# A graph attention layer on one core: differences of destinations, from two GpSimd subtractions to twenty-one ScalarE activations

## The chip, the core and the metric

The kernel runs on one core of a Trainium2 chip. The metric is the device time of one execution in microseconds. The engines are named as in the profile: PE (TensorE, matrix products), DVE (VectorE), ACT (ScalarE), POOL (GpSimd) and SP (SyncE, which here only issues DMA transfers). Each engine works through its own list of instructions in order; semaphores make it wait for another engine or for a transfer. The 16 DMA engines serve the queues of all issuers. The gathers by index are issued by POOL, which spends time on each; nearly all other transfers are issued by SP.

## What is computed

There are 12,500 nodes with 128 features and 400,000 edges, sorted by destination, with 32 features each. Cut to what matters:

```python
h = relu(layernorm(x))                       # no weights
def layer(x, src, dst, edge_attr):           # x is h; 8 heads of 16 channels
    y = ln(x, ln1_g, ln1_b)
    x_l, x_r, e = y @ W_l, y @ W_r, edge_attr @ W_e
    m = leaky_relu(x_l[src] + x_r[dst] + e, 0.2)
    alpha = einsum('ehc,hc->eh', m, att)     # softmax over the edges of a destination
    a = softmax_by(dst, alpha)
    h2 = x + segment_sum(x_l[src] * a, dst) + bias
    return h2 + gelu(ln(h2, ln2_g, ln2_b) @ W1 + b1) @ W2 + b2
out = x + layer(h, src, dst, edge_attr)
```

Each node also has an edge to itself, whose features are the mean over all edges. Everything is float32, except where the kernel uses bf16 for numbers that fit it or for parts of numbers.

## The kernel before, in words

Nodes are taken in 25 quads: 24 of four tiles of 128 nodes, and a last one of two tiles. Edges are taken in 782 pairs. A pair is two units, a unit is 256 edges.

**The node phase** (lines 690 to 744) is a software pipeline of 35 rounds. In each round a table of stages runs for different quads: x_stats (DVE) for quad r, relu (ACT) for quad r-3, h_turn (PE) for r-4, h_square (ACT) and the copy out of PSUM for r-5 (even quads by ACT, odd by DVE), product (PE) for r-7, and x_l (DVE, then a store to xl_dram by SP) for r-8. The rows of x_l stand in three SBUF buffers in turn (xls), so the x_l of a quad waits until the store of three quads before has landed. At the head of a round stand a reciprocal (DVE) for the roots of two rounds ago and a square root (ACT) for those of the last round. first_xr does the same for x_r of the first quad, one step a round from round 8 on; two of its steps are L580 and L586 on DVE. All is recorded in program order, and this order is kept on each engine: nothing is rescheduled.

**Raw gathers.** 24 of the edge pairs get their source rows in another way: in the node phase POOL gathers rows of the input x for them (raw_gather, L270, four gathers of 128 rows a pair), SP stores them in raw_dram (raw_store, L278, three rounds on), and in the edge phase they are turned into rows of x_l. The round of each is in rows_at (L720): 5/4 of its number, and three rounds more from the tenth on. There are five raw tiles in turn, so a gather waits for the store of five pairs before. The position in rows_at does not change the order on POOL, which has nothing else to do here except the subtractions; it sets where the stores stand in SP's list among the stores of x_l (L535).

**Differences.** The edge phase places edges by the difference of their destination from the first destination of their unit, and from that of their pair. dc holds all destinations, 112 partitions of 3,584 (14 units, or 7 pairs) and a few beyond. In round 12 from_first converts them to float32 (L389) and POOL takes both sets of differences, each in one instruction over the whole tile with the first destinations broadcast (L393); SP stores each in DRAM (L399). In round 14 fits (L401) tests on DVE whether the windows used later suffice and sets a flag, by which the kernel chooses between the edge phase described here and a general one.

**The edge phase** (window_edges) runs 782 rounds. For each pair POOL gathers four blocks of 128 rows of xl_dram (gather, L896), four rounds ahead, into 12 buffers; SP loads edge features, differences (dlw, L913) and a window of x_r; DVE compares differences with a column (L924); PE forms the sum z, ACT and DVE bend it, PE and DVE and ACT make scores and weights, and PE sums weighted rows. Finished nodes are normalised and put through the feed-forward part between rounds. Before its first gather POOL clears six buffers (L875). As these lie in memory that the node phase used, and as the gathers read xl_dram, the node phase's gathers and the stores to xl_dram have to have landed by then.

Of the kernel before, what the change touches and what calls it, by code (L numbers as in the profile page):

```python
# [13 lines left out]
F32 = mybir.dt.float32  # L14
BF16 = mybir.dt.bfloat16
I32 = mybir.dt.int32
AF = mybir.ActivationFunctionType
OP = mybir.AluOpType
# [16 lines left out]
U = KU * P  # L35
UP = 2
QP = 4
RU = 14
# [80 lines left out]
def raw_pairs(nt, n_edges):  # L119

    n_pr = -(-n_edges // (UP * U))
    at = [xr_round(t, nt, n_edges) + XR_STEPS + 1 for t in range(GN, nt, GN)]
    return [(r + RAW_STEPS + AHEAD + 1, r) for r in at if r + RAW_STEPS + AHEAD + 2 < n_pr]
# [11 lines left out]
def tile_gnn(  # L135
# [23 lines left out]
    nc = tc.nc  # L159
# [8 lines left out]
    RP = -(-NU // RU)  # L168
# [12 lines left out]
    dc_dram = dram.tile([RP * RU * U], BF16, name="dc_dram")  # L181
    du_dram = dram.tile([RP * RU * U], BF16, name="du_dram")
    raw = [{"c": c, "i": i, "round": r, "n": UP * KU} for i, (c, r) in enumerate(raw_pairs(NT, n_edges))]
# [36 lines left out]
    rng = pre.enter_context(tc.tile_pool(name="rng", bufs=1))  # L220
# [9 lines left out]
    EP = RU * U  # L230
# [4 lines left out]
    def load_weights():  # L235
        nc.scalar.dma_start(wl_sb, w_l)
        nc.scalar.dma_start(wr_sb, w_r)
        nc.scalar.dma_start(g1_c, column(ln1_g))
        nc.scalar.dma_start(b1n_c, column(ln1_b))

    def load_consts():
        for i, v in enumerate((ln2_g, ln2_b, None, b1[0:P], b1[P : 2 * P])):
            if v is not None:
                nc.sync.dma_start(cols[:, 2 + i : 3 + i], column(v))
        nc.sync.dma_start(att_c, bass.AP(tensor=att.tensor, offset=att.offset, ap=[[1, C], [C, H], [1, 1]]))
        nc.sync.dma_start(we_sb, bass.AP(tensor=w_e.tensor, offset=w_e.offset, ap=[[P, DE], [0, QP], [1, P]]))
        nc.sync.dma_start(w1_sb, w1)
        nc.sync.dma_start(w2_sb, w2.rearrange("(k p) f -> p k f", p=P))
        nc.sync.dma_start(bias_r, row_bcast(bias, P))
        nc.sync.dma_start(b2_r, row_bcast(b2, P))  # L250
        nc.sync.dma_start(src_sb, src)
        nc.sync.dma_start(first_sb, bass.AP(tensor=dst.tensor, offset=dst.offset, ap=[[0, 1], [U, NU]]))
# [3 lines left out]
    def load_raw():  # L256
        step = raw[1]["c"] - raw[0]["c"]
        assert all(d["c"] == raw[0]["c"] + i * step for i, d in enumerate(raw))
        nc.sync.dma_start(
            src_raw,  # L260
            bass.AP(
                tensor=src.tensor, offset=src.offset + raw[0]["c"] * UP * KU,
                ap=[[NCH * K, P], [step * UP * KU, len(raw)], [1, UP * KU]],
            ),
        )

    def raw_gather(d):
        d["x"] = node.tile([P, UP * KU, P], F32, name="raw", bufs=5)
        for j in range(d["n"]):
            nc.gpsimd.indirect_dma_start(  # L270
                out=d["x"][:, j, :],
                out_offset=None,
                in_=x,
                in_offset=bass.IndirectOffsetOnAxis(ap=src_raw[:, d["i"], j : j + 1], axis=0),
            )

    def raw_store(d):
        nc.sync.dma_start(raw_dram[d["i"], :, 0 : d["n"], :], d["x"][:, 0 : d["n"]])  # L278

    def load_x(t0, n):  # L280
        if n > 0:
            nc.sync.dma_start(h_sb[:, t0 : t0 + n, :], x_t[:, t0 : t0 + n, :])  # L282

    def load_dst():
        nc.gpsimd.memset(dc[:, EP : EP + U + 1], NO_NODE)
        if rest < EP:
            nc.gpsimd.memset(dc[(RP - 1) // DE * DE :, rest:EP], NO_NODE)
        if RP > 1:
            over = min(EP + U + 1, NCH * CE - (RP - 2) * EP)
            nc.sync.dma_start(  # L290
                dc[0 : RP - 1, 0:EP], bass.AP(tensor=dst.tensor, offset=dst.offset, ap=[[EP, RP - 1], [1, EP]])
            )
            nc.sync.dma_start(
                dc[RP - 2 : RP - 1, EP:over],
                bass.AP(tensor=dst.tensor, offset=dst.offset + (RP - 1) * EP, ap=[[0, 1], [1, over - EP]]),
            )
            if RP > 2:
                nc.sync.dma_start(
                    dc[0 : RP - 2, EP : EP + U + 1],
                    bass.AP(tensor=dst.tensor, offset=dst.offset + EP, ap=[[EP, RP - 2], [1, U + 1]]),  # L300
                )
        nc.sync.dma_start(dc[RP - 1 : RP, 0:rest], dst[(RP - 1) * EP :].rearrange("(o e) -> o e", o=1))
        nc.gpsimd.memset(lu, NO_NODE)
        if RP > 1:
            nc.sync.dma_start(
                lu[0 : RP - 1, :], bass.AP(tensor=dst.tensor, offset=dst.offset + U - 1, ap=[[EP, RP - 1], [U, RU]])
            )
        nc.sync.dma_start(
            lu[RP - 1 : RP, 0 : rest // U],
            bass.AP(tensor=dst.tensor, offset=dst.offset + (RP - 1) * EP + U - 1, ap=[[0, 1], [U, rest // U]]),  # L310
        )

        u = NUE - 1
        nc.sync.dma_start(
            lu[u // RU : u // RU + 1, u % RU : u % RU + 1],
            bass.AP(tensor=dst.tensor, offset=dst.offset + n_edges - 1, ap=[[0, 1], [1, 1]]),
        )
# [27 lines left out]
    def count_up():  # L345
        iota(nc, nh, [[-1, H], [-H, NW]], 0, 1)
        iota(nc, own, [[-1, NW], [0, H]], -NC3, 1)
        iota(nc, last, [[0, NW], [0, H]], -NC3 - NW, 1)
        iota(nc, third, [[-NS, CW]], 0, 1)
        iota(nc, in_order, [[1, CW]])  # L350
        iota(nc, unit, [[0, 1]], -NC3, 1)
        iota(nc, fq, [[-1, QP], [-QP, DE]], 0, 1)
        iota(nc, place, [[1, RU]], 0, RU)
        iota(nc, fh, [[-1, H], [-H, C]], 0, 1)
# [29 lines left out]

    df = rng.tile([RP, EP + U + 1], F32, name="df")
    bad = rng.tile([RP, 2], F32, name="bad")

    def from_first():
        nc.vector.tensor_copy(df, dc)  # L389
        for step, to in ((U, du_dram), (UP * U, dc_dram)):  # L390
            de = df[:, 0:EP].rearrange("p (u e) -> p u e", e=step)
            dlb = rng.tile([RP, EP], BF16, name="dlb", bufs=2)
            nc.gpsimd.tensor_tensor(  # L393
                dlb.rearrange("p (u e) -> p u e", e=step),
                de,
                de[:, :, 0:1].to_broadcast([RP, EP // step, step]),
                op=OP.subtract,
            )
            nc.sync.dma_start(to.rearrange("(p e) -> p e", e=EP), dlb)  # L399

    def fits():  # L401
# [44 lines left out]
    qs = [  # L446
        {"t0": t, "n": n, "ts": slice(t, t + n), "h": h_sb[:, t : t + n, :], "mean": mean_sb[:, t : t + n]}
        for t, n in quads
    ]
# [253 lines left out]
    LAST = 8  # L703
    first_xr = xr_steps(node, lambda: once_ps.tile([P, GN * P], F32, name="w_ps"))
    with tc.manual_schedule():
        make_identity(nc, ident)
        count_up()
        for t in xls:
            nc.gpsimd.memset(t[:, :, P:], 1.0)
        load_weights()  # L710
        load_x(0, min(GN, NT))
        load_raw()
        load_x(GN, min(3 * GN, NT - GN))
        for t in range(4 * GN, NT, 14):
            load_x(t, min(14, NT - t))
        load_dst()
        load_consts()
        nc.gpsimd.memset(empty, 0.0)
        nc.gpsimd.memset(empty[:, :, C + 1 : SH], CAP)
        rows_at = [i * 5 // 4 + (3 if i >= 10 else 0) for i in range(len(raw))]  # L720
        for r in range(max(max(len(qs), 9) + LAST + 1, rows_at[-1] + 4)):
            for d, at in zip(raw, rows_at):
                if r == at:
                    raw_gather(d)
                if r == at + 3:
                    raw_store(d)
            if r == 3:
                weights()
            if r == 7:
                edge_constants()  # L730
            if r == 12:
                from_first()
            if r == 14:
                fits()
            for t in slots(r - 2):
                nc.vector.reciprocal(t, t)
            for t in slots(r - 1):
                nc.scalar.activation(t, t, AF.Sqrt)
            for late, f in node_stages:
                if 0 <= r - late < len(qs):  # L740
                    f(qs[r - late], r)
            if 0 <= r - LAST < len(first_xr):
                first_xr[r - LAST](qs[0])
        clear(0)
# [952 lines left out]
```

## Time and profile before

| | |
|---|---|
| time, median of 3 runs | 4050.42 us (4048.72 to 4051.7) |
| profiled execution, its own time | 4055.89 us |
| its span, first to last instruction | 4053.7 us |
| mean granted clock of TensorE | 0.955 |
| busy: PE, DVE, ACT, POOL | 3555.2 us (88%), 2539.5 (63%), 2135.2 (53%), 2984.9 (74%) |
| chain that ended last: PE, POOL, DMA | 40%, 24%, 22% of the span |
| DMA traffic | 560.85 MB, mean 138 GB/s |
| the two subtractions of L393 | 12.3 us on POOL, at 100.5 and 106.7 us |
| raw gathers (L270) | 96 of 995 ns on average |
| edge gathers (L896) | 3029, 949 ns on average |

The rows that the profile gives for groups of instructions name a line, an engine, an operation and a tile, then count, busy time, the mean of one in ns, and the idle time of the engine just ahead of them with what ended it ("issue" where the profile shows no wait). A timeline row is the start in us, the duration in us, engine, line, operation, output and input; in square brackets stands the idle time ahead of it and who ended it. Start-to-start distances are of more use than durations where instructions of an engine overlap a little. Rows with SPq are transfers as SP issues them: their duration is that of issuing, not of the transfer.

### The profile page before, as it was taken

The numbers are of one execution on the slowest core, as the hardware profiler recorded it, in microseconds if no ns is written. First come the engines' busy times: TensorE is split into PE (matmuls) and PEld (weight loads), VectorE is DVE, ScalarE is ACT, GpSimd is POOL, SyncE is SP. The second block draws the span as 40 slices with busy tenths as digits, with TensorE's granted clock in tenths as the row PEclk, the third lists the DMA queues.
The fourth block names the chain that finished last, engine by engine and source line by source line (L and its number), as shares of the span: only waits on it lengthen the run. The fifth ranks groups of instructions, "written<-read, shape, count | busy, mean of one in ns | idle before, by whom it ended". The sixth has DMA issues, their size and how long they took to land.

```text
span 4053.7 us, 65778 instructions
## 1 busy us (share of the span) xinstructions
PE 3555.2 (88%) x19254; PEld 2501.5 (62%) x19255; DVE 2539.5 (63%) x5834; ACT 2135.2 (53%) x4638; POOL 2984.9 (74%) x3156
## 2 busy tenths in 40 slices
PE   2388888998989999999999999999989999989986
PEld 2356665665666666666666666666766666666664
DVE  5656665766666666666666666666666665666654
ACT  4544444544445555565455556555555555545543
POOL 4777777777777777777777777777777777777772
PEclk6699999999999999999999999999999999999998
DMA  5668878777766666656665665656666666565562
GB/s 160 198 165 198 185 194 197 171 163 165 172 124 126 126 124 131 123 121 129 132 125 124 128 129 120 136 123 117 124 136 126 124 130 128 107 135 114 120 134 50
DMA packets 648212, 560.85 MB, mean 138 GB/s; under 512 B 386387, under 2 KB 525506, under 8 KB 647602
## 3 DMA queue, kind: packets, MB, share of 16 engines
q1 hardware_dynamic: 547266, 339.01, 33.7%
q0 software_dynamic: 100000, 217.41, 30.2%
q8 instruction: 156, 2.56, 0.3%
q14 instruction: 214, 1.75, 0.2%
q10 hardware_dynamic: 576, 0.13, 0.0%
HBM read 489.81 MB, written 66.32 MB: 137 GB/s over the span
## 4 chain that ended last, share of the span: by engine, by line
PE 40%; POOL 24%; DMA 22%; issue 13%; SPq 1%; DVE 0%; ACT 0%; POOLq 0%; DVEq 0%; ACTq 0%
POOL xs L896 22%; DMA xs<-xl_dram,src_sb 21%; PE z L942 9%; PE acc L1000 8%; PE ab L960 7%; PE pt_ps L986 4%; PE z L938 4%; PE z L941 2%; PE ab L959 2%; POOL raw L270 2%; PE acc L1233 1%; PE acc L1208 1%; DMA lu<-in_dst 1%; SPq L282 0%; DMA state<-rec 0%
## 5 line engine op out<-in xcount | busy, mean ns | idle before, releaser
L896 POOL DMA_INDIRECT xs<-xl_dram,src_sb x3029 | 2873.0, 949 | 923.2 <-issue 796.0
L978 ACT ACTIVATE p<-ab,rec 128x256 f32<-128x256 f32 x1563 | 656.8, 472 | 1056.5 <-DVE rec L967 1044.3
L1009 DVE TENSOR_TENSOR own<-acc,diag 128x272 f32<-128x272 f32 x782 | 344.1, 440 | 1068.5 <-PE acc L1000 1039.6
L938 PE MATMUL z<-ident,xs 128*128 128x128 f32 x3125 | 573.3, 283 | 353.0 <-DMA xs<-xl_dram,src_sb 318.3
L938 PEld LDWEIGHTS z<-ident,xs 128*128 128x128 f32 x3125 | 399.5, 142 | 772.3 <-DMA xs<-xl_dram,src_sb 434.5
L1000 PE MATMUL acc<-xs,pt 128*128 128x136 f32 x6250 | 874.9, 284 | 0.2 <-DVE f_yo L1247 0.2
L942 PE MATMUL z<-ea,we_z 128*128 128x512 f32 x1564 | 835.4, 617 | 0.0
L1000 PEld LDWEIGHTS acc<-xs,pt 128*128 128x128 f32 x6250 | 802.6, 195 | 0.4 <-PE pt_ps L986 0.4
L960 PE MATMUL ab<-m,negrep 128*128 128x512 f32 x1564 | 801.4, 594 | 0.0
L991 ACT COPY pt<-pt_ps 128x512 f32<-128x512 f32 x782 | 455.9, 583 | 623.3 <-PE pt_ps L986 611.5
L986 PEld LDWEIGHTS pt_ps<-ident,p 128*128 128x128 f32 x3125 | 407.8, 146 | 438.2 <-issue 386.4
L967 DVE TENSOR_REDUCE rec<-ab 128x2 f32<-128x512 f32 x781 | 540.2, 692 | 123.4 <-PE ab L960 113.2
L953 DVE TENSOR_TENSOR m<-z,zs 128x512 f32<-128x512 f32 x782 | 533.0, 682 | 115.0 <-ACT zs L948 114.7
L948 ACT ACTIVATE zs<-z 128x512 f32<-128x512 f32 x782 | 472.2, 604 | 41.4 <-DMA dlw<-dc_dram 33.6
L986 PE MATMUL pt_ps<-ident,p 128*128 128x128 f32 x3125 | 489.2, 281 | 2.2 <-ACT pt L991 1.3
L1015 DVE TENSOR_REDUCE rec<-own 128x34 f32<-128x272 f32 x782 | 340.9, 436 | 26.7
L942 PEld LDWEIGHTS z<-ea,we_z 128*128 128x128 f32 x1564 | 306.5, 196 | 32.5
L960 PEld LDWEIGHTS ab<-m,negrep 128*128 128x128 f32 x1564 | 300.6, 192 | 37.1 <-issue 1.2
L941 PE MATMUL z<-ne,xrw 128*128 128x512 bf16 x782 | 304.0, 389 | 0.2 <-DMA xs<-xl_dram,src_sb 0.2
L959 PE MATMUL ab<-ne,farw 128*128 128x512 bf16 x782 | 299.6, 383 | 0.0
L924 DVE TENSOR_SCALAR ne<-dlw,nid 112x512 bf16<-112x512 bf16 x782 | 289.8, 371 | 13.0 <-DMA dlw<-du_dram 13.0
L270 POOL DMA_INDIRECT raw<-in_x,src_raw x96 | 95.5, 995 | 71.3 <-DMA raw_dram<-raw 40.1
(198 smaller groups left out, 2235.6 us busy)
## 6 DMA issues: line engine op xcount, KB each, us to landing
dlw<-dc_dram SPq DMA_DIRECT2D x196, 384.0 KB
ea<-in_ea_t SPq DMA_DIRECT2D x196, 256.0 KB
ea_s<-in_ea_t SPq DMA_DIRECT2D x98, 512.0 KB
xs<-xl_dram,src_sb POOLq DMA_INDIRECT x3029
state<-rec SPq DMA_DIRECT2D x1563, 9.0 KB
xrw<-xs_dram SPq DMA_DIRECT2D x782, 24.0 KB
state<-empty SPq DMA_DIRECT2D x28, 504.0 KB
st<-state SPq DMA_DIRECT2D x48, 288.0 KB
```

Of the source, the lines that this page charges most:

```text
L896: nc.gpsimd.indirect_dma_start(out=xs[:, j, :], out_offset=None, in_=xl_dram, in_offset=bass.IndirectOffsetOnAxis(ap=src_sb[:, c * KP + j ...
L938: nc.tensor.matmul(z[:, j * P : (j + 1) * P], d["xs"][:, j, 0:P], ident, start=(j == 0), stop=False, is_transpose=True)
L941: nc.tensor.matmul(z[:, :e], xrw[c % NV], d["ne"][:, :e], start=False, stop=False)
L942: nc.tensor.matmul(z[:, :e], we_z[:, c % QP, :], d["ea"][:, :e], start=False, stop=True)
L948: nc.scalar.activation(d["zs"][:, :e], d["z"][:, :e], AF.Copy, scale=SLOPE)
L953: nc.vector.tensor_tensor(d["m"][:, :e], d["z"][:, :e], d["zs"][:, :e], op=OP.max)
L960: nc.tensor.matmul(ab[:, :e], negrep.rearrange("p n h -> p (n h)"), d["m"][:, :e], start=False, stop=True)
L967: nc.vector.tensor_reduce(d["rec"][:, :, CX], d["ab"].rearrange("p (u e) -> p u e", e=U), AX.X, OP.min)
L978: nc.scalar.activation(d["p"][:, us], d["ab"][:, us], AF.Exp, bias=d["rec"][:, i, CX:SH], scale=-1.0)
L986: nc.tensor.transpose(d["pt_ps"][:, js], d["p"][:, js], ident)
L991: nc.scalar.copy(d["pt"][:, :e], d["pt_ps"][:, :e])
L1000: nc.tensor.matmul(d["acc"][:, i, :], d["pt"][:, j * P : (j + 1) * P], d["xs"][:, j, :], start=(j == js[0]), stop=(j == js[-1]),)
```

## The change

The float32 destinations are made as before. One DVE instruction then puts the negated first destination of each unit in a column of a small tile nf. In rounds 13 to 19 differ has ACT compute, for two units and one pair a round, destination plus that column (activation Identity with a bias per partition) into one of two bf16 tiles: two instructions over 112x256 and one over 112x512 in each round, at the head of ACT's work of the round. In round 20 keep_differences stores both tiles as before. The extra three rounds in rows_at from the tenth raw pair on are gone, and the loop over rounds has a bound for the new steps; it now runs 34 rounds.

```diff
     df = rng.tile([RP, EP + U + 1], F32, name="df")
     bad = rng.tile([RP, 2], F32, name="bad")
+    nf = rng.tile([RP, RU], F32, name="nf")
+    dlbs = [rng.tile([RP, EP], BF16, name=f"dlb{i}") for i in range(2)]
 
     def from_first():
         nc.vector.tensor_copy(df, dc)
-        for step, to in ((U, du_dram), (UP * U, dc_dram)):
-            de = df[:, 0:EP].rearrange("p (u e) -> p u e", e=step)
-            dlb = rng.tile([RP, EP], BF16, name="dlb", bufs=2)
-            nc.gpsimd.tensor_tensor(
-                dlb.rearrange("p (u e) -> p u e", e=step),
-                de,
-                de[:, :, 0:1].to_broadcast([RP, EP // step, step]),
-                op=OP.subtract,
-            )
+        nc.vector.tensor_scalar(nf, df[:, 0:EP:U], -1.0, None, op0=OP.mult)
+
+    def differ(i):
+        for dlb, step, us in ((dlbs[0], U, range(UP * i, UP * i + UP)), (dlbs[1], UP * U, (i,))):
+            for u in us:
+                es = slice(u * step, (u + 1) * step)
+                f = u * step // U
+                nc.scalar.activation(dlb[:, es], df[:, es], AF.Identity, bias=nf[:, f : f + 1])
+
+    def keep_differences():
+        for dlb, to in zip(dlbs, (du_dram, dc_dram)):
             nc.sync.dma_start(to.rearrange("(p e) -> p e", e=EP), dlb)
...
-        rows_at = [i * 5 // 4 + (3 if i >= 10 else 0) for i in range(len(raw))]
-        for r in range(max(max(len(qs), 9) + LAST + 1, rows_at[-1] + 4)):
+        rows_at = [i * 5 // 4 for i in range(len(raw))]
+        for r in range(max(max(len(qs), 9) + LAST + 1, 14 + RU // UP, rows_at[-1] + 4)):
...
             if r == 12:
                 from_first()
+            if 0 <= r - 13 < RU // UP:
+                differ(r - 13)
+            if r == 13 + RU // UP:
+                keep_differences()
             if r == 14:
                 fits()
```

Lines from L402 on stand some lines lower after the change (eight at the end of the file), so L896 before is L904 after.

## The prediction, made before the result was known

> **What bounds the kernel now.** I first read the page's table of groups, to see which engine has work without a gap, then the table by stretches for that engine's costliest line, then the timelines of POOL, DVE, ACT and SP from 70 to 190 us, where the changed code runs.
>
> The group, from the page, and its stretches (columns: the stretch, its length, POOL's busy time in that line with its count, clock, DMA share, GB/s):
>
> ```profile
> L896 POOL DMA_INDIRECT xs<-xl_dram,src_sb x3029 | 2873.0, 949 | 923.2 <-issue 796.0
> ```
>
> ```profile
> 600.00:1000.00 400.00, 302.68 (x320) 0.97 0.75 174
> ...
> 3400.00:3800.00 400.00, 302.89 (x319) 0.97 0.63 125
> ```
>
> POOL shows as 74% busy, but its idle time is nearly all "issue", and the longest single wait that the table of waits gives for L896 is 0.3 us. It issues 320 gathers per 400 us in every stretch, 1.25 us each, whatever the other engines do. From the first gather at 186.38 us to the end of the last at 3982.5 that is 3796.1 us for 3029 gathers, 1.253 us apiece. So the edge phase is as long as its train of gathers, and PE, with the larger busy share, only follows it; behind the last gather come 4053.7 - 3982.5 = 71 us. **The time is set by when the first edge gather starts.** What sets that is the node phase, on POOL:
>
> ```profile
> 99.57 0.95 POOL L270 DMA_INDIRECT raw<-in_x,src_raw  x1 [0.30 <-issue]
> 100.55 12.28 POOL L393 TENSOR_TENSOR dlb<-df 112x3584 bf16<-112x3584 f32 x2
> 112.98 1.23 POOL L270 DMA_INDIRECT raw<-in_x,src_raw  x1 [0.16 <-issue]
> 114.52 0.94 POOL L270 DMA_INDIRECT raw<-in_x,src_raw  x1 [0.30 <-issue]
> ...
> 181.96 0.94 POOL L270 DMA_INDIRECT raw<-in_x,src_raw  x1 [0.30 <-issue]
> 185.29 0.94 POOL L875 MEMSET xrw<- 128x128 bf16 x6 [2.39 <-DMA raw<-in_x,src_raw]
> 186.38 0.95 POOL L896 DMA_INDIRECT xs<-xl_dram,src_sb  x1 [0.15 <-POOL xrw L875]
> ```
>
> Seen here: the 76 raw gathers after 71.47 us run back to back, the two subtractions sit in the middle of them, and the edge phase begins when the last raw gather has landed. ACT is done with the node phase at 166.3 and DVE at 170.3, so POOL is last by 12 us.
>
> **The change, part by part.**
>
> *Two subtractions leave POOL.* 2 x 6.16 = 12.3 us. Without them the gather at 112.98 starts at 99.57 + 1.25 = 100.82, the next at 102.07 instead of 114.52, and with 1.25 us each the last starts 12.45 us earlier, at 169.5. All of it lies on the path. POOL stays ahead of its buffers: a raw tile's next gather needs the store of five tiles before, and in my ledger every such store has landed more than 15 us before POOL asks for it.
>
> *DVE comes free too.* Beside the subtractions stands
>
> ```profile
> 101.42 11.97 DVE L586 TENSOR_TENSOR xr_parts<-xr,xr_parts 128x512 bf16<-128x512 f32 x1
> ```
>
> while the same shape with one operand in PSUM (L580) took 0.68 us. [...] ACT paid for it:
>
> ```profile
> 99.91 0.21 ACT L738 ACTIVATE roots_sb<-roots_sb 128x8 f32<-128x8 f32 x1 [5.18 <-DVE roots_sb L473]
> ...
> 115.67 0.21 ACT L738 ACTIVATE roots_sb<-roots_sb 128x8 f32<-128x8 f32 x1 [11.64 <-DVE roots_sb L473]
> ```
>
> [...]
>
> *Twenty-one activations on ACT*: in each of rounds 13 to 19 two of 112x256 and one of 112x512, bias from a column. No row shows them. Start to start, the 128x128 square with a bias column (L507) takes 0.29 us, the 128x512 cast out of SBUF (L583) 0.52, the 128x512 Identity with both columns (L559) 0.66, the 128x256 exponential (L978) 0.42. So 112x256 lies between 0.29 and 0.48, 112x512 between 0.52 and 0.66: a round costs 1.1 to 1.6 us, I take 1.4, and seven 9.8 us (7.7 to 11.3). [...] Ledger: round 13 starts at 86.5 as now; rounds 13 to 15 (+1.4 each) fall into ACT's 5.18 us wait, so round 15 ends near 104 as now; round 16 follows at once instead of after 11.64 us; rounds 16 to 19 (4 x 1.4 + 3.6 + 4.0 + 3.6 + 4.0) end at 124.9 instead of 133.4. ACT ends at 157.8 instead of 166.3, DVE's last x_l follows by 162 to 166 (it needs a buffer whose store waits on SP). Queued behind each group are the roots, relus and squares of its round, and behind those PE's turns and products. The slot that counts, below, is at 173, so ACT has some 7 us to spare; beyond that each us costs one. Identity brings no table load: L549 and L559 run between the square roots, and ACT's only load before 200 us is the one at 2.70. ACT's wait for nf at round 13 costs nothing: df ends at 83.1 on DVE, nf is one 112x14 instruction of 0.17 us (as L417), and ACT gets there at 86.5.
>
> *Stores.* The two stores of differences (784 KB each) move in SP's queue from 106.7 and 112.9 us to round 20, about 125 us; their reader starts near 178. SP no longer stands still from 90.2 to 106.7 and to 112.9. DVE's 2.79 us wait for an xl store at 118.43 goes with it.
>
> *Raw stores three rounds earlier from the tenth on.* They are only queued earlier, past three x_l stores each; POOL's order is the same. On SP a raw store waits for its gather, so x_l stores now stand behind it. By POOL's pace raw store i can go at about 58 + 5i us, and DVE asks for the x_l buffer three rounds on; until the last rounds that is 5 to 15 us later. At the end it bites. Now:
>
> ```profile
> 175.28 0.34 SPq L278 DMA_DIRECT2D raw_dram<-raw  x1
> 175.72 0.39 SPq L535 DMA_DIRECT2D xl_dram<-xl  x1
> 179.62 5.33 SPq L278 DMA_DIRECT2D raw_dram<-raw  x2
> 185.00 1.14 SPq L685 DMA_DIRECT2D state<-empty  x2
> ```
>
> the last x_l store leaves 9 us before the last raw store. In the changed program the last raw store is queued ahead of the last two x_l stores, and the first edge gather reads what these write. **This is the new wait.** The last raw gather starts at 169.5, its store can go 2.65 us later (181.96 to 184.60 now), 172.2; the x_l stores at 172.6 and 173.1. For their landing two rows are near: the x_l store at 165.91 freed DVE at 169.68, 3.8 us; the one at 175.72 moved its last bytes at 178.4, 2.7 us. I take 3.3: landed at 176.4 (175.8 to 176.9); POOL's memsets and its step to the first gather take 1.1 us (185.29 to 186.38) and the return from the wait about 0.1 more. First edge gather at 177.6 instead of 186.4, 8.8 us earlier; one more DVE piece beside the gathers (L586 now running) may hold one for 0.1. Edge loads on SP come about 10 us earlier, so they do not become the limit; PE waits for gathers from 218 us on either way.
>
> **Sum.** -12.4 + 3.7 = -8.7 us. The profiled execution took 4055.89 us (span 4053.7), so 4047.2 on its terms. The median of the runs shown is 5.5 lower, 4050.42; I take the same difference from it: **4041.7 us**.
>
> **Rivals.**
> - *The whole 12.4 us* (4038.0; 0.18): the x_l stores land as fast as the last gather is seen by all queues, or DMA, without gathers beside it, is quicker than in either row. For: the queues are emptier there than at 165 us. Against: three transfers of 672 KB together stand in one queue.
> - *A slower tail* (4044.6; 0.16): the last raw gather lands in 3.9 us, as the one of 166.96 did (store at 170.85), and x_l in 5.1 us, as from 113.28 to 118.43: 1.25 + 1.8 us more than my values, gain 5.8. For: both are rows. Against: both had more traffic beside them.
> - *Slower* (0.04): the gathers of the edge phase lose their pace. A gather beside a long DVE instruction was held (3.76 us beside L404, 2.49 beside L389, instead of 0.94), and the mean of L896 is 949 ns against a usual 944: 15 us of holding in all. If the shifted start doubled it: -8.7 + 15, 4056.7. It decides from 2.9 ns per gather on. Against: 320 per 400 us in all stretches.
> - *No effect* (0.02): another wait than POOL's holds the start, 4050.4.
>
> The forecast itself has 0.60, with its own range 4040 to 4043.5. With the outer cases the range is **4036.8 to 4046.0**. About 0.2%, 8.1 us, can be told from no change; my 8.7 lies just beyond it. Of the forecast's 0.60 some 0.41 lie beyond 8.1, with the first rival 0.59 faster; the rest of it, the slower tail and no effect make 0.37; slower 0.04.
>
> **What would show it.** POOL: raw gathers without a gap, the last at about 169.5; a wait ahead of the memsets that ends with an xl store, not a raw gather; the first edge gather at 177 to 178; still 320 gathers per 400 us. DVE: L586's instruction at 0.7 us. ACT: 21 new activations of 9.8 us in all, the wait of 11.6 us gone, its node work done near 158. It is wrong if ACT ends after 165, if a raw gather waits for a store, or if the first gather starts later than 181.

## The result, and the profile after

The changed kernel takes **4041.15 us** (median of 12 runs, 4038.58 to 4046.41), the kernel before, beside it on the same chip, 4050.03 (12 runs, 4047.63 to 4053.25). The ratio is 0.9978 with an interval of 0.997 to 0.9987: 8.9 us faster, between 5.3 and 12.2. The forecast was 4041.7.

The edge phase first. From the table of groups, and then two of its eight stretches (columns as before):

```profile
L904 POOL DMA_INDIRECT xs<-xl_dram,src_sb x3029 | 2868.7, 947 | 923.2 <-issue 792.5
```

```profile
600.00:1000.00 400.00, 302.75 (x320) 0.97 0.74 174
3400.00:3800.00 400.00, 302.44 (x321) 0.98 0.60 123
```

The train of edge gathers has not changed: 320 in 400 us, 947 ns each (949 before). So what changed must have happened ahead of it. POOL's timeline where the node phase ends:

```profile
170.13 0.94 POOL L270 DMA_INDIRECT raw<-in_x,src_raw  x1 [0.30 <-issue]
177.02 0.93 POOL L883 MEMSET xrw<- 128x128 bf16 x6 [5.95 <-DMA xl_dram<-xl]
178.11 0.95 POOL L904 DMA_INDIRECT xs<-xl_dram,src_sb  x1 [0.16 <-issue]
```

The last raw gather starts at 170.13 instead of 181.96, 11.8 us earlier. But the wait behind it, which was 2.39 us for a raw gather, is now 5.95 us for a store of x_l. The first edge gather starts at 178.11 instead of 186.38, 8.3 us earlier. What this wait stands on is in the chain that ended last, here its main pieces between 170 and 177 us (start, duration, what):

```profile
170.13 2.66 DMA raw<-in_x,src_raw
172.94 0.34 SPq L278
173.37 0.39 SPq L539
173.84 2.69 DMA xl_dram<-xl
```

The last raw gather lands, its store goes, behind it the stores of x_l go, and only when those have landed may POOL go on. On ACT's timeline, the two roots that stood behind its long waits before (5.18 and 11.64 us), and between them one round of the differences:

```profile
100.55 0.21 ACT L746 ACTIVATE roots_sb<-roots_sb 128x8 f32<-128x8 f32 x1 [1.27 <-DVE roots_sb L477]
...
104.58 1.52 ACT L399 ACTIVATE dlb<-df,nf 112x256 bf16<-112x256 f32 x3
106.00 0.20 ACT L746 ACTIVATE roots_sb<-roots_sb 128x8 f32<-128x8 f32 x1
```

Three activations take 1.42 us from the start of the first to the start of what follows. Of the waits ahead of L746, 1.27 us of the first is left and nothing of the second.

The profiled execution became 14.5 us shorter in span (4053.7 to 4039.2), more than the medians: 8.3 us are the earlier start, 4.4 are the train (3796.1 to 3791.7 us for the same 3029 gathers) and 1.9 the tail behind it. In the twelve traces of this study the train takes between 3791 and 3798.5 us, in no order that follows an edit, so these 4.4 us are not counted as a gain of the change. So the start of the first edge gather is the sharper measure of the node phase, and the medians have to agree with it.

### The profile page after: what moved, and what is told of

Same layout as the page of the kernel before. It is cut to its first block, busy times and chain, and to the rows that moved or that the text cites. A ratio compares the mean times of both kernels' runs of the same rounds, so it can differ in the third digit from the quotient of the medians.

```text
span 4039.2 us, 65602 instructions
## 1 busy us (share of the span) xinstructions
PE 3540.4 (88%) x19059; PEld 2496.8 (62%) x19255; DVE 2531.2 (63%) x5835; ACT 2144.4 (53%) x4659; POOL 2968.2 (73%) x3154
## 4 chain that ended last, share of the span: by engine, by line
PE 37%; POOL 25%; DMA 23%; issue 13%; SPq 1%; DVE 1%; ACT 0%; POOLq 0%; DVEq 0%; ACTq 0%
POOL xs L904 23%; DMA xs<-xl_dram,src_sb 22%; PE z L950 8%; PE acc L1008 8%; PE ab L968 7%; PE z L946 4%; PE pt_ps L994 4%; PE z L949 2%; POOL raw L270 2%; PE ab L967 1%; PE acc L1241 1%; DMA lu<-in_dst 1%; PE acc L1216 1%; SPq L282 0%; PE acc L1111 0%
## 5 line engine op out<-in xcount | busy, mean ns | idle before, releaser
L904 POOL DMA_INDIRECT xs<-xl_dram,src_sb x3029 | 2868.7, 947 | 923.2 <-issue 792.5
L968 PE MATMUL ab<-m,negrep 128*128 128x512 f32 x1564 | 799.9, 593 | 10.7 <-issue 0.7
L949 PE MATMUL z<-ne,xrw 128*128 128x512 bf16 (+1 forms) x781 | 303.4, 388 | 0.2 <-DMA ea_s<-in_ea_t 0.2
L967 PE MATMUL ab<-ne,farw 128*128 128x512 bf16 x588 | 225.7, 384 | 0.3 <-ACT p L986 0.2
L270 POOL DMA_INDIRECT raw<-in_x,src_raw x96 | 95.4, 994 | 71.9 <-DMA raw_dram<-raw 40.7
```

Source lines behind the costliest of these rows:

```text
L904: nc.gpsimd.indirect_dma_start(out=xs[:, j, :], out_offset=None, in_=xl_dram, in_offset=bass.IndirectOffsetOnAxis(ap=src_sb[:, c * KP + j ...
L949: nc.tensor.matmul(z[:, :e], xrw[c % NV], d["ne"][:, :e], start=False, stop=False)
L968: nc.tensor.matmul(ab[:, :e], negrep.rearrange("p n h -> p (n h)"), d["m"][:, :e], start=False, stop=True)
```

## The experiments

The theory was the prediction's own: time follows the start of the first edge gather; POOL's 12.3 us bring it forward, and the order of the stores at the end takes some 3.7 back. The rivals: the gain comes from DVE and ACT, which no longer stand still beside the subtractions; the order of the stores does nothing, or does all; ACT's new work costs its length.

Ten runs, in three batches, each on one chip with its own runs of the kernel before: 4058.05, 4051.43 and 4048.99 us. Since these differ by 9 us, as much as the effect, each kernel is compared only with the runs beside it. The columns in the middle come from the traces, in us from the start; those of the kernel before were not traced again, so 186.38 from the first trace stands for all.

| kernel | last raw gather starts | ACT's last node root | first edge gather | against 186.38 | median | against before beside it | ratio, interval |
|---|---|---|---|---|---|---|---|
| before | 181.96 | 166.1 | 186.38 | | 4050.03 | | |
| changed | 170.13 | 158.2 | 178.11 | -8.3 | 4041.15 | -8.9 | 0.997 to 0.9987 |
| e1 changed, old order of stores | 169.82 | 157.7 | 174.19 | -12.2 | 4045.26 | -12.8 | 0.9958 to 0.9981 |
| e2 before, new order of stores | 181.88 | 171.6 | 189.70 | +3.3 | 4061.86 | +3.8 | 1.0002 to 1.002 |
| e3 changed, POOL kept busy | 182.07 | 170.1 | 189.84 | +3.5 | 4060.25 | +2.2 | 0.9995 to 1.0014 |
| e4 changed, ACT's work twice | 171.13 | 166.2 | 178.97 | -7.4 | 4048.47 | -9.6 | 0.9968 to 0.9986 |
| e5 before, subtractions early | 171.85 | 161.2 | 176.20 | -10.2 | 4040.89 | -10.5 | 0.9964 to 0.9984 |
| e6 changed, stores six rounds on | 169.71 | 157.6 | 174.19 | -12.2 | 4037.03 | -14.4 | 0.9949 to 0.9976 |
| e7 changed, ACT's work three times | 172.61 | 175.8 | 183.64 | -2.7 | 4048.26 | -3.2 | 0.9983 to 1.0001 |
| e8 changed once more | 170.09 | 158.2 | 177.92 | -8.5 | 4040.21 | -11.2 | 0.9961 to 0.9984 |
| e9 changed, first raw stores early | 150.46 | 156.2 | 163.21 | -23.2 | 4027.14 | -21.9 | 0.993 to 0.9957 |
| e10 as e6 | 169.83 | 157.7 | 174.21 | -12.2 | 4038.06 | -10.9 | 0.996 to 0.9982 |

In every row the change of the time is that of the first edge gather to within 2.8 us, over changes from -23 to +4. That is the theory's first half. The rest says what moves the first edge gather.

**e1, the old order of the stores.**

```diff
-        rows_at = [i * 5 // 4 for i in range(len(raw))]
+        rows_at = [i * 5 // 4 + (3 if i >= 10 else 0) for i in range(len(raw))]
```

> The changed kernel, with the raw stores back at their old rounds (three rounds later from the tenth pair on). Theory (the start of the first edge gather sets the time, and the order of the stores at the end of the node phase takes 3.7 us of the gain back): the last raw gather starts at about 170 us as in the changed kernel, the x_l stores stand ahead of the last raw stores and no wait of POOL ends with an x_l store any more; first edge gather at about 174.5 us instead of 178.1, time 3.5 us below the changed kernel, about 4037.5 us, 12.4 below the kernel before. Rival (the order of the stores makes no difference, or was needed): first gather at 178 and the time of the changed kernel, 4041, or more.

POOL's timeline of e1:

```profile
169.82 0.95 POOL L270 DMA_INDIRECT raw<-in_x,src_raw  x1 [0.30 <-issue]
173.10 0.93 POOL L883 MEMSET xrw<- 128x128 bf16 x6 [2.34 <-DMA raw<-in_x,src_raw]
174.19 0.95 POOL L904 DMA_INDIRECT xs<-xl_dram,src_sb  x1 [0.16 <-issue]
```

SP's timeline of e1 at the same place:

```profile
164.49 0.39 SPq L539 DMA_DIRECT2D xl_dram<-xl  x1
167.71 5.05 SPq L278 DMA_DIRECT2D raw_dram<-raw  x2
```

The last store of x_l leaves at 164.5, before the last raw stores, and the wait is again 2.34 us for a raw gather. The first edge gather comes 3.9 us before the changed kernel's. Against the kernel before the whole 12.2 us of the subtractions are there, and 12.8 in time. The absolute 4037.5 of the expectation missed, because on this chip the kernel before, too, took 8 us longer (4058.05 against 4050.03); against the runs beside it, it held.

**e2, the new order of the stores alone.** The kernel before, with the line of the diff above the other way round.

> The kernel before, with only the raw stores three rounds earlier; the differences stay two subtractions on GpSimd. Theory: the raw gathers are as before, the last at about 182 us, and the x_l stores then stand behind its store; first edge gather at about 190 us instead of 186.4, time 3.7 us above the kernel before, about 4053.7 us. Rival (the new order of stores brings the gain, by itself): 4041 to 4046 us, first gather before 182. Rival (the order makes no difference): 4050.

POOL's timeline of e2:

```profile
181.88 0.95 POOL L270 DMA_INDIRECT raw<-in_x,src_raw  x1 [0.31 <-issue]
188.61 0.94 POOL L875 MEMSET xrw<- 128x128 bf16 x6 [5.78 <-DMA xl_dram<-xl]
189.70 0.95 POOL L896 DMA_INDIRECT xs<-xl_dram,src_sb  x1 [0.15 <-POOL xrw L875]
```

The last raw gather stays where it was, and the same 5.8 us wait for a store of x_l appears: +3.3 us at the gather, +3.8 in time, interval 0.8 to 8. So of the two parts of the change one gains 12 us and the other loses between 3 and 4. The rival that the order brings the gain is out, and so is the one that it does nothing. e2 had a side effect: SP stands from 90 to 118 us behind the stores of the differences, with x_l stores behind them. ACT waits 19.1 us and ends at 171.6, 5.5 later than in the kernel before; it is still hidden behind POOL's 181.9.

**e3, POOL as busy as before.**

```diff
     nf = rng.tile([RP, RU], F32, name="nf")
+    scratch = rng.tile([RP, EP], F32, name="scratch")
...
         nc.vector.tensor_scalar(nf, df[:, 0:EP:U], -1.0, None, op0=OP.mult)
+        for _ in range(4):
+            nc.gpsimd.memset(scratch, 0.0)
```

> The changed kernel, with four clears of an unused tile of 112x3584 float32 on GpSimd where the two subtractions stood. They only write, so that they should not hold DVE as the subtractions did. Theory (POOL's own time is what the change saved): the last raw gather moves by the length of the four clears, estimated at 11 to 12 us in all, and so do the first edge gather and the time: about 4053 us; DVE's product of x_r keeps its 0.7 us and ACT has no long wait. Rival (the gain came from DVE and ACT, which stood still beside the subtractions): the time of the changed kernel, 4041, though POOL is as busy as before.

POOL's timeline of e3:

```profile
105.73 12.53 POOL L395 MEMSET scratch<- 112x3584 f32 x4
...
189.84 0.95 POOL L907 DMA_INDIRECT xs<-xl_dram,src_sb  x1 [0.15 <-POOL xrw L886]
```

The clears took 12.53 us together, and the first edge gather came 11.7 us later than in the changed kernel. In time e3 is 2.2 us over the kernel before (interval -2 to 5.7, so not told from it) where the changed kernel is 8.9 to 11.2 under it: 11 to 13 us. The theory's number came out, but the experiment told less apart than it was meant to. DVE's timeline beside the first clear:

```profile
105.76 0.16 DVE L483 SCALAR_TENSOR_TENSOR n_m<-n_stats,roots_sb 128x4 f32<-128x4 f32 x1
105.84 3.02 DVE L495 TENSOR_SCALAR mean_sb<-mean_sb 128x4 f32<-128x4 f32 x1
```

L483 has two inputs in SBUF and runs in 0.16 us beside a clear, as the expectation had it. But the next, L495, one input and 4 columns, normally 0.16 us, takes 3.02 us and ends when the first of the four clears does (105.73 plus a quarter of 12.53 is 108.86). The same comes back at each of the other three: a tensor_scalar (L480, L495, L480) takes 1.69, 2.81 and 1.69 us and ends within 0.05 us of the end of a clear. That clears, which only write, would not hold DVE was the author's assumption, and these four rows are against it. So DVE stood still here too, for 9 of the 12.5 us, and e3 by itself does not separate POOL's time from DVE's. e4 does.

**e4 and e7, ACT's work twice and three times.**

```diff
             if 0 <= r - 13 < RU // UP:
-                differ(r - 13)
+                for _ in range(2):
+                    differ(r - 13)
```

In e7 it is range(3).

> The changed kernel, with every difference computed twice on ACT (42 activations instead of 21, the same results): 9.9 us more on ACT. Theory (the activations are hidden behind POOL's raw gathers, with 7 us or more to spare and each us beyond that costing one): ACT's node work ends at about 168 us, the last x_l is ready close to 173, when its place in the queue comes; 0 to 3 us above the changed kernel, 4041 to 4044. Rival (ACT's work costs its length, now hidden in the gain): 10 us above the changed kernel, 4051.

> The changed kernel, with every difference computed three times on ACT (63 activations, the same results): 19.8 us more on ACT than in the changed kernel. Doubling them moved ACT's end by 7.9 us (158.35 to 166.23) and the first edge gather by 0.9. Theory (hidden up to the place of the last x_l stores in SP's queue, at 173.4 us; beyond that each us costs one): ACT ends at about 176, the last x_l is ready at about 179.5, 6 us past its place; first edge gather at about 184, 6 us (4 to 8) above the changed kernel. Rival (ACT's work is hidden whatever its length): not over 2 us. Rival (it costs its length): 20 us.

POOL's timeline of e4:

```profile
171.13 0.95 POOL L270 DMA_INDIRECT raw<-in_x,src_raw  x1 [0.30 <-issue]
177.88 0.94 POOL L884 MEMSET xrw<- 128x128 bf16 x6 [5.80 <-DMA xl_dram<-xl]
178.97 0.95 POOL L905 DMA_INDIRECT xs<-xl_dram,src_sb  x1 [0.15 <-issue]
```

ACT's, DVE's and SP's timelines of e4, one row each:

```profile
166.23 0.20 ACT L747 ACTIVATE roots_sb<-roots_sb 128x2 f32<-128x2 f32 x1 [0.21 <-DVE roots_sb L516]
```

```profile
169.41 0.61 DVE L531 SCALAR_TENSOR_TENSOR xl<-lr,roots_sb,bl_r 128x128 f32<-128x128 f32 x2 [0.69 <-DMA xl_dram<-xl]
```

```profile
174.25 1.00 SPq L539 DMA_DIRECT2D xl_dram<-xl  x2
```

In e4 ACT's last root is at 166.2, within 0.2 us of where it was in the kernel before (166.1), DVE's last x_l ends at 170.0 (170.3 before), and the gain is there (-9.6 us). That takes the first rival out: ACT and DVE need not be any earlier for it. The 0.9 us at the first gather come from POOL's own gathers (the last raw one is 1.0 us later), not from x_l, whose store has its place in the queue only at 174.3, behind the last raw store.

Three times is past the place. e7, DVE's last x_l, then POOL's timeline:

```profile
178.42 0.61 DVE L531 SCALAR_TENSOR_TENSOR xl<-lr,roots_sb,bl_r 128x128 f32<-128x128 f32 x2
```

```profile
182.56 0.93 POOL L884 MEMSET xrw<- 128x128 bf16 x6 [9.00 <-DMA xl_dram<-xl]
183.64 0.95 POOL L905 DMA_INDIRECT xs<-xl_dram,src_sb  x1 [0.16 <-issue]
```

The last x_l does not wait for its buffer any more; it goes as soon as ACT and PE let it and ends at 179.0, and POOL waits 9.0 us. The first edge gather is 5.7 us behind that of the changed kernel run beside it (177.92), in time 8.1 us (4048.26 against 4040.21, and no run of the one reaches the other's). That is what the expectation had (about 184 us, 4 to 8 us above). So neither rival holds: ACT's work is free up to a point, and what lies beyond it counts in full. The first 9.9 us added cost about 1 us; the next 9.9 made the first edge gather 4.7 us later than in e4, where the last x_l ends 4.8 us past the place of 174.3 (the time became 6.4 us longer, each set against the kernel before beside it). ACT's delay also reached POOL's own train here: two raw gathers waited for a raw store, 1.6 and 2.1 us, so that the last of them starts 2.5 us later than in e8, at 172.6; the wait for x_l covers that.

**e5, the subtractions left on GpSimd, but early.** The kernel before with one call moved:

```diff
+            if r == 6:
+                from_first()
             for d, at in zip(raw, rows_at):
...
-            if r == 12:
-                from_first()
```

> The kernel before, with its conversion and its two GpSimd subtractions put six rounds earlier, ahead of the gathers of that round, so that they fall into the 40 us in which POOL waits for the first raw store (31 to 72 us). ACT has no differences to compute. Theory (POOL's time between 72 us and the first edge gather is what counts, whoever does the work): last raw gather at about 170 us, the old order of the stores, first edge gather at about 174, 12.4 us below the kernel before and 3.5 below the changed one. It is less if the destinations land so late that the subtractions run past 72 us: each us of that costs one. Rival (the move to ACT is what counts): the time of the kernel before.

POOL's timeline of e5:

```profile
51.75 12.28 POOL L393 TENSOR_TENSOR dlb<-df 112x3584 bf16<-112x3584 f32 x2 [20.40 <-DVE roots_sb L736]
...
71.79 0.96 POOL L270 DMA_INDIRECT raw<-in_x,src_raw  x1 [7.76 <-DMA raw_dram<-raw]
...
125.75 0.94 POOL L270 DMA_INDIRECT raw<-in_x,src_raw  x1 [1.21 <-DMA raw_dram<-raw]
...
138.15 0.94 POOL L270 DMA_INDIRECT raw<-in_x,src_raw  x1 [2.72 <-DMA raw_dram<-raw]
```

DVE's timeline of e5, beside the subtractions:

```profile
51.78 6.15 DVE L476 SCALAR_TENSOR_TENSOR n_m<-n_stats,roots_sb 128x4 f32<-128x4 f32 x1
...
57.92 6.13 DVE L512 TENSOR_SCALAR roots_sb<-n_ssq 128x4 f32<-128x4 f32 x1
```

The same 12.28 us of subtractions now lie in POOL's 40 us wait, which ends at 71.8 as before. The first edge gather is 10.2 us earlier, the time 10.5 us lower: as good as the changed kernel, with ACT doing none of it. DVE is not spared either: two instructions of usually 0.16 us took 6.15 and 6.13 beside the subtractions, together as long as L586 had. It is held at another time, and its last x_l ends 4.7 us earlier than in the kernel before; but the gain does not need DVE to be free of the subtractions. What is missing from the expected 12.4 is in the last two of POOL's rows: POOL, now ahead of the rounds in which raw stores are recorded, waits twice for one, 3.9 us; and 1.5 us come back, since no raw gather stands beside DVE's conversion any more (2.49 us instead of 0.94 in the kernel before). So what matters is not that ACT does the work but where it stands in POOL's list.

**e6 and e10, raw stores six rounds on.** In the changed kernel:

```diff
-        for r in range(max(max(len(qs), 9) + LAST + 1, 14 + RU // UP, rows_at[-1] + 4)):
+        for r in range(max(max(len(qs), 9) + LAST + 1, 14 + RU // UP, rows_at[-1] + 7)):
...
-                if r == at + 3:
+                if r == at + 6:
                     raw_store(d)
```

> The changed kernel, with every raw store recorded six rounds after its gather instead of three, the early ones too. Theory: as the x_l stores stand ahead of the last raw stores, no x_l store waits at the end; first edge gather at about 174 us, 3.5 us below the changed kernel and 12.4 below the kernel before. But the first raw stores go later as well, by three rounds: if that moves POOL's restart (71.9 us now) by more than POOL can win back, each us of it costs one. Rival (the order of the stores makes no difference): the time of the changed kernel.

> The changed kernel with every raw store six rounds after its gather, once more, beside the last experiment on the same chip. Theory: first edge gather at 174.2 us, 3.7 us below the changed kernel and 12 us below the kernel before.

The first edge gather starts at 174.19 and 174.21, as in e1, 3.7 us before that of e8, and the wait ahead of it is again one for a raw gather (2.45 and 2.34 us); e6's time is 3.2 us below that of e8, which ran beside it. In e6 POOL's restart stays at 71.5 (71.9 in the changed kernel, where SP comes to the first raw store only at 59 us). Against the kernel before, e6 has -14.4 and e10, the same kernel, -10.9: that is how much the medians of such batches scatter.

**e9, the head of the raw train.** POOL's 40 us wait, seen in the changed kernel, on SP's timeline:

```profile
25.96 25.32 SPq L308 DMA_DIRECT2D lu<-in_dst  x1
...
59.27 10.27 SPq L278 DMA_DIRECT2D raw_dram<-raw  x5
```

The first raw store stands behind the loads of destinations, and the issue of one of these lasts 25 us. In e9 it stands ahead of them:

```diff
-        load_dst()
         load_consts()
+        for d in raw[:5]:
+            raw_gather(d)
+        for d in raw[:5]:
+            raw_store(d)
+        load_dst()
...
-            for d, at in zip(raw, rows_at):
-                if r == at:
+            for i, d in enumerate(raw[5:], 5):
+                keep = i + 2 if i < 19 else 22 + 2 * (i - 19)
+                if r == keep - 3:
                     raw_gather(d)
-                if r == at + 3:
+                if r == keep:
                     raw_store(d)
```

> The changed kernel, with the first five raw pairs gathered and stored ahead of the loads of destinations (the constants are loaded ahead of them too), and the later raw gathers and stores placed by the time at which POOL could then do them. POOL now waits from 31 to 72 us for the first raw store, because SP issues it only after these loads, one of which holds SP's queue for 25 us. Theory (POOL's train of raw gathers sets the first edge gather as long as ACT and DVE are done earlier): POOL resumes at about 50 us, the last raw gather starts at about 150, and then the node phase on ACT (end 158) and the last x_l (161 and a store of some 4 us) are late next: first edge gather at about 166 us, 12 us below the changed kernel. It is less if the later destinations or the stores placed earlier hold the x_l stores up; with ACT ending over 170 the gain is gone. Rival (POOL's start is not what counts): the time of the changed kernel.

POOL's timeline of e9:

```profile
43.27 0.95 POOL L270 DMA_INDIRECT raw<-in_x,src_raw  x1 [11.00 <-DMA raw_dram<-raw]
...
76.99 0.94 POOL L270 DMA_INDIRECT raw<-in_x,src_raw  x1 [9.05 <-DMA raw_dram<-raw]
...
150.46 0.94 POOL L270 DMA_INDIRECT raw<-in_x,src_raw  x1 [0.30 <-issue]
162.13 0.93 POOL L888 MEMSET xrw<- 128x128 bf16 x6 [10.72 <-DMA xl_dram<-xl]
163.21 0.95 POOL L909 DMA_INDIRECT xs<-xl_dram,src_sb  x1 [0.15 <-issue]
```

POOL resumes at 43 instead of 72 us, waits once more for a raw store behind the delayed load, and is done with raw gathers at 151, ahead of ACT (156.2). The first edge gather starts at 163.2, the time is 4027.14: 0.9943 of the kernel before, 21.9 us less, where the changed kernel had 8.9 and 11.2. The expectation, 12 us below the changed kernel with the first edge gather at 166, holds (POOL resumed 7 us earlier than it had, and the first edge gather came 3 us earlier), and e9 is better than both kernels of the change. The last wait is now 10.7 us for x_l, and DVE's last x_l goes without any wait for its buffer, so ACT, PE and DVE are late next, as the expectation had it. Here the 9.9 us that ACT took over would stand on the path. That is read from the trace; no run took them away.

## Why the prediction was right

**What bounds it: right.** Every one of the eleven comparisons moved with the first edge gather. The pace stayed, 320 gathers per 400 us, and the tail too, but for 1.9 us, so the rival on the slower side had no place. (It put the holding of gathers at 15 us, from a usual 944 ns; the median in that trace is 945, which makes it 12.)

**-12.45 us for the two subtractions: right, a little too high.** The last raw gather moved by 11.8: forecast at 169.5, found at 170.13. Of the 0.6 us, 0.4 is POOL's restart (71.87 against 71.47 us), and 0.3 the gather that runs beside DVE's test of windows (4.05 instead of 3.76 us). e1 shows the whole amount at the end of the chain, 12.2 us. POOL stayed ahead of its buffers, as forecast, but not everywhere by the 15 us of the ledger: the sixteenth raw store is issued at 138.46, 13 us before the gather at 151.40 that needs its tile.

**DVE comes free too: right.** L586's instruction, 11.97 us beside the subtractions, is now

```profile
102.06 0.68 DVE L590 TENSOR_TENSOR xr_parts<-xr,xr_parts 128x512 bf16<-128x512 f32 x1
```

and 0.68 us was forecast as 0.7. ACT's two waits of 5.18 and 11.64 us became 1.27 and none. That the gain does not depend on it is e4: with ACT back at 166.2 the gain stays.

**Twenty-one activations, 9.8 us: 9.9 measured.** Six rounds took 1.40 to 1.43 us from start to start; behind the seventh stands ACT's wait of 1.27 us, and it is taken as 1.42. That lies between the row-based ends of 1.1 and 1.6; the pieces have 0.51 us (112x256) and 0.72 (112x512) each, overlapping by some 0.1. What fewer and wider activations would have taken no run shows; that ACT's time was not what counted is shown by e4. ACT's last node root was forecast at 157.8 and stands at 158.15.

**"ACT has some 7 us to spare; beyond that each costs one": the place right, the size too small.** 7.9 us more (e4) cost nothing from x_l, and the last x_l then still came 4.3 us before its store's place (ended at 170.0, place at 174.3). So about 12 us were to spare, and e7 gives the same: ACT ended 17.7 us later than in e8 and the first edge gather came 5.7 us later. The term that was off is the last x_l at 162 to 166 us: in the changed kernel it starts at 166.89, but what it waits for is a buffer, not ACT:

```profile
166.89 0.61 DVE L531 SCALAR_TENSOR_TENSOR xl<-lr,roots_sb,bl_r 128x128 f32<-128x128 f32 x2 [3.23 <-DMA xl_dram<-xl]
```

The buffer's store stands behind a raw store that waits for its gather. A wait of this kind gives way when ACT gets slower (0.69 us in e4, none in e7), so the distance from ACT's end to the slot is the better measure of spare time than the distance from the last x_l.

**Stores of the differences: right, but for what came in their place.** In SP's queue they leave at 128 us instead of 107 and 113, and DVE's wait of 2.79 us at 118 is gone; the two of 3.1 and 3.2 us ahead of the last x_l are new.

**Raw stores three rounds earlier, the new wait: right in kind and size.** Forecast: last raw store at 172.2, x_l behind it, landing 3.3 us after the last is issued, first edge gather at 177.6, 3.7 us given back. Found: 172.94, two stores from 173.37, POOL free at about 177.0, first edge gather at 178.11; each step 0.5 to 0.8 us later than forecast, as the last raw gather itself was 0.6 us late. What it gives back is 3.9 us by e1, 3.7 by e6 and e8, and +3.3 on its own in e2.

**Sum: -8.7 forecast, -8.9 and -11.2 measured** in two batches, and -8.3 and -8.5 at the first edge gather. The rival of the whole 12.4 us is the kernel of e1 and e6, with another order of stores; that of the slower tail would have needed a first edge gather near 181. (Its three transfers are 664 KB together, not 672: 256, 272 and 136.) The mechanism and its two terms were right, each to within 0.7 us. That the median came within 0.6 us of the forecast is in part luck: the same kernel set against other runs of the kernel before gave 8.9 and 11.2 us, and e6 and e10, one kernel, 14.4 and 10.9.

## What to carry to other kernels

Find the train that runs without a gap to the end, and judge an edit by what it does to that train's first instruction; which engine takes the work over matters only up to the spare time at the place where its result is next needed, and then each microsecond costs one (in e7 4.8 us past the place, and a first edge gather 4.7 us later than in e4). Work that stands in the middle of a train can as well go into a wait of the same engine: e5 got the gain of the change (10.5 us) without a second engine. In SP's queue here a store that waited for its producer held all behind it, at the end (3.7 us here) and at the head, where POOL stood idle for 40 us behind slow loads that had nothing to do with its raw gathers (11 us and, further on, another 9 once e9 had put the stores ahead of them): ask of each queue what stands behind a transfer that waits.

## What the runs showed of the hardware

A GpSimd clear of 112x3584 float32, which reads nothing, held DVE's single-input float32 tensor_scalar until it ended (3.02 us instead of 0.16 in e3), while a scalar_tensor_tensor with two SBUF inputs beside the same clear took its usual 0.16. The same scalar_tensor_tensor (n_m, L483 in e3 and L476 in e5) took 6.15 us in e5 beside a subtraction, whose operands GpSimd reads from SBUF. In the kernel before, L586 took 11.97 us and ended 0.6 us after the second of the two subtractions, while in e5 each held instruction (6.15 and 6.13 us) was let go after one; what decides that, no run shows.

The reverse also shows: the raw gather that POOL issues while DVE runs its 3.88 us test over two SBUF operands takes four times as long as usual. The changed kernel, DVE's timeline and then POOL's:

```profile
91.47 3.88 DVE L408 CUSTOM_DVE_ANT_0 junk<-df 112x3584 f32<-112x3584 f32 x1
```

```profile
92.12 4.05 POOL L270 DMA_INDIRECT raw<-in_x,src_raw  x1 [0.30 <-issue]
```

The gather ends 0.8 us after the test does, 0.94 being its usual length. In the kernel before it takes 3.76 us and ends 0.8 us after the test too, and in e1 to e9 one gather of that part of the train takes 3.49 to 4.69 us. Together with the one beside the conversion (2.48 us in the changed kernel) that is 4.6 us of POOL's train in the node phase, which no run here took away whole; e5 took away the second.

SP's issue of L308 lasted 25.32 us in the changed kernel and 26.98 in e9, where it stands 20 us later. It is a load of 8 numbers; ahead of it in the queue stands L305, a load of 1,554 single numbers of 4 bytes. That SP waits there for the many small pieces of L305, and not for the traffic of that time, fits the two durations (16 to 17 ns a number, an estimate from them), but no run changed that load.
